# Second attention: products of q's rows, and of k's positions for the last two batches, on VectorE instead of GpSimd, at other steps

## The chip, the cores and the metric

The kernel runs on one core of a Trainium2 chip. The metric is the device time of one execution in microseconds (us), lower is better. The engines are called as in the profile: PE (TensorE, with PEld for its weight loads), ACT (ScalarE), DVE (VectorE), POOL (GpSimd) and SP (SyncE, which here issues most DMAs). Each engine works through its own list of instructions in order and waits at the head of the list until what that instruction needs is there.

## The reference

The input `x` has 4 batches of 512 positions with 128 features. There are two layers, each of the form

```
xn = layernorm(x)
s  = attention(xn)
g  = silu(ffn(xn))
x  = x + s * g
```

The first layer has a segmented linear attention with memory (16 heads of 64) and a mixture of 8 experts. The second layer, which the change touches, has 16 heads of 8 features and 16 "wavelength" channels:

```
Q, K, V = projections of xn, per head 8 features
for each channel w:
    scores = (Q * cos_pm[w]) @ (K * cos_pm[w])^T * scale     # times a cosine that is 1 here
    acc += softmax(scores) @ V * interference_weights[w]
s = (acc / 16) @ Wo + bo
```

followed by an expert layer with gelu (8 experts, the two best per position).

## The kernel before

All of it is one program: loads and first expert layer, first attention, second expert layer, second attention, and a path for large values that isn't taken here. The change lies in the second attention and in what is prepared for it.

**How the second attention computes.** The 16 channels differ only in a factor on the scores. So the kernel computes two exponential functions of the scores for every pair of positions (`e`, and its square), and adds the low powers of the scores (first, second, third), from which every channel's exponential is put together as a weighted sum. The part over pairs of positions is long: exponentials on ACT (`function1` with f = 0), squares on ACT or DVE (f = 1), and the sums over keys on PE (`acc`). The powers need no pairs: sums over keys of products of k's features (the "forms", `pl`) are multiplied with products of q's features (`first`, `second`, `third`, into `b`).

**The loop of `attn1`.** There are 64 steps, 16 per batch; step t of batch b is `i = 16 b + t`. A step takes one tile of 128 keys for four heads with all 512 queries. In each step PE sums over keys with the two functions of this step (`acc`, 16 matmuls), then computes the scores two steps ahead (`s`, 4 matmuls), then does one or two extra pieces of work. ACT computes the exponentials of the next step and evicts small results; the squares of the next step follow. The extra pieces are the preparation of the batch after this one (`prepare1`) and the mixing of the channels of this or the last batch (`sums1` with `den` and `inv`, `quotients1` with `mix` and `pr`, `bank1` with `b`, `output1` with `po`). Their matmuls are issued in one step, what follows on other engines (called `rest`) in the next; a `rest` may return a function that is done one step later still. All these instructions are pinned in the order in which the program writes them, engine by engine.

**Squares on DVE.** `RELIEVED` lists the steps (mod 16) whose second half of squares is done by DVE instead of ACT; the first tuple is for batches 0 to 2, the second for the last batch. The square of step i+1 is issued in step i. The functions of step 0 of batch 0 are done ahead, in `opening1`, which is called from within the second expert layer, before its last two groups of expert sums (`g`, line 966). For lack of other space they lie in `third1` and `first1[1]`.

**Preparation of k.** `tokens("k")` projects k with positions on partitions. DVE adds the bias (`tokk`), POOL copies the 8 features behind themselves (`twice`, 128 x 512) and multiplies them into `feat`, all products of two features, in two instructions of 128 x 2048 (line 1229). DVE's `cubes(m)` makes products of three features from it (lines 1311 to 1323) for four groups of heads; PE's `forms(m)` (`pl`) sums both. For batches 0 and 1 `tokens("k")` runs during the second expert layer; for batches 2 and 3 in steps 12 (PE) and 13 (the rest) of batches 0 and 1. There is one `feat`, and one set of cubes at a time (`feat3`).

**Products of q.** q's rows are written to DRAM in expanded form (`qe`, `qf`) and loaded again as `first`, `second` and `third`, with features on partitions, for two halves of the heads (mm = 0, 1). `quads1` multiplies `second` with `first` (line 1447) on POOL, in two instructions of 128 x 512 per half; `cubes1` then multiplies `first` with `second` and `third` with `second` on DVE (lines 1456, 1458), and `bank1` uses all three at steps 8 and 15. A table in `attn1` gives the steps at which each is loaded (`load`, `other`), squared (`two`) and cubed (`three`, `four`); a negative step lies in the batch before.

**Other work on POOL in the loop:** splitting k and q into three bf16 parts (`partk`, `leftk`, `partq`, `leftq`, ten instructions per batch of 0.6 to 1.6 us each), the squares of `tokq`, the gate (`th`, `g`), the sums of `pr`, and the output `y`. SP issues the writes of the parts and of q's expanded rows and all loads, in program order.

## Time and profile before

| | |
|---|---|
| time, median of 3 runs | 775.9 us (772.36 to 778.27) |
| the profiled execution | 776.21 us |
| its span, first to last instruction | 774.4 us |
| mean granted clock of PE | 0.986 |
| second attention's loop | 475.9 to 751.7 us, then the end |
| POOL, `second` (line 1447) | 32 instructions, 55.3 us |
| POOL, `feat` (line 1229), within the loop | 4 instructions, 17.7 us |
| DVE, `first` (line 1456) | 16 instructions, mean 1857 ns, shortest 1189 ns |

The profile is of one execution. A row of a group gives the line, engine and operation, out<-in by the program's names, the shapes and the count, then the busy time in us and the mean of one in ns, then how long the engine was idle before these instructions and what ended that. The timeline gives start and length in us and the idle time before in brackets. In the table by windows each line has the window, its length, the busy time and number of instructions of PE, PEld, DVE, ACT and POOL, the granted clock, the busy share of the DMA engines and GB/s.

### The profile page before, as it was taken

The numbers are of one execution on the slowest core, as the hardware profiler recorded it, in microseconds if no ns is written. First come the engines' busy times: TensorE is split into PE (matmuls) and PEld (weight loads), VectorE is DVE, ScalarE is ACT, GpSimd is POOL, SyncE is SP. The second block draws the span as 40 slices with busy tenths as digits, with TensorE's granted clock in tenths as the row PEclk, the third lists the DMA queues.
The fourth block names the chain that finished last, engine by engine and source line by source line (L and its number), as shares of the span: only waits on it lengthen the run. The fifth ranks groups of instructions, "written<-read, shape, count | busy, mean of one in ns | idle before, by whom it ended". The sixth has DMA issues, their size and how long they took to land. (4 is left out here: it accounts for less than half of the span.)

```text
span 774.4 us, 23667 instructions
## 1 busy us (share of the span) xinstructions
PE 727.4 (94%) x10060; PEld 437.9 (57%) x10060; DVE 523.2 (68%) x1111; ACT 489.3 (63%) x793; POOL 361.9 (47%) x378
## 2 busy tenths in 40 slices
PE   8999899999999989799999999999789987999997
PEld 4665577787787858666776774343234332432235
DVE  7775476656558766864455535877897699676964
ACT  4332666767668776544322227999688786879940
POOL 7660045555546435653063041734971776170650
PEclk9999999999999999999999999999899998999997
DMA  7830423213123121000013802667856393639200
GB/s 191 151 80 0 120 75 99 80 48 98 52 66 95 39 76 40 21 2 1 1 39 111 219 2 68 192 177 169 197 169 153 99 244 135 149 94 218 55 16 17
DMA packets 77745, 74.72 MB, mean 96 GB/s; under 512 B 41937, under 2 KB 66801, under 8 KB 74561
## 3 DMA queue, kind: packets, MB, share of 16 engines
q1 hardware_dynamic: 75568, 71.98, 35.6%
q0 software_dynamic: 1488, 0.90, 0.8%
q8 instruction: 81, 1.33, 0.8%
q10 hardware_dynamic: 576, 0.26, 0.1%
q14 instruction: 32, 0.25, 0.1%
HBM read 50.04 MB, written 23.07 MB: 94 GB/s over the span
## 5 line engine op out<-in xcount | busy, mean ns | idle before, releaser
L334 ACT ACTIVATE e<-s 128x1024 f32<-128x1024 f32 x126 | 123.5, 1048 | 25.9 <-PE s L331 25.1
L331 PE MATMUL acc<-e,strip 128*32 128x512 f32 x1008 | 127.6, 611 | 0.3 <-DVE e L1687 0.3
L334 ACT ACTIVATE e<-e 128x1024 f32<-128x1024 f32 x99 | 102.4, 1088 | 0.0
L334 ACT ACTIVATE h<-ph 128x1024 f32<-128x1024 f32 x32 | 32.8, 1025 | 84.2 <-PE ph L331 84.2
L769 POOL TENSOR_TENSOR t<-t,gate 128x512 f32<-128x512 f32 x32 | 40.8, 1275 | 72.1 <-DVE sums L768 65.7
L1447 POOL TENSOR_TENSOR second<-second,first 128x512 f32<-128x512 f32 x32 | 55.3, 1752 | 29.8 <-DMA second<-qf 22.8
L331 PEld LDWEIGHTS acc<-e,strip 128*32 128x32 f32 x1008 | 28.8, 111 | 71.1 <-issue 61.6
L331 PEld LDWEIGHTS eo<-w_out,h 128*128 128x128 f32 x512 | 60.7, 192 | 12.5 <-issue 9.6
L331 PE MATMUL eo<-w_out,h 128*128 128x128 f32 x512 | 63.4, 277 | 1.6 <-DVE g L966 1.3
L334 ACT ACTIVATE pj<-pp 128x512 f32<-128x512 f32 x64 | 38.3, 598 | 39.4 <-PE pp L331 39.1
L679 DVE SCALAR_TENSOR_TENSOR elu<-elu,up 128x512 f32<-128x512 f32 x60 | 48.9, 815 | 20.2 <-ACT up L334 20.1
L331 PE MATMUL ph<-xnT,w_in 128*128 128x512 f32 x128 | 60.3, 594 | 0.0
L731 POOL TENSOR_TENSOR t<-t,gate 128x512 f32<-128x512 f32 x32 | 41.4, 1295 | 39.9 <-DVE t L712 39.8
L966 DVE SCALAR_TENSOR_TENSOR g<-eo,gw,g 128x128 f32<-128x128 f32 x112 | 31.4, 342 | 40.1 <-PE eo L331 40.1
L1687 DVE TENSOR_TENSOR e<-e 128x1024 f32<-128x1024 f32 x27 | 42.0, 1556 | 19.1 <-ACT e L334 19.0
L770 POOL TENSOR_TENSOR t<-t,t 128x512 f32<-128x512 f32 x32 | 46.1, 1439 | 2.5
L331 PE MATMUL s<-q,k 64*128 64x512 bf16 x256 | 39.8, 382 | 2.9 <-ACT e L334 1.5
L331 PEld LDWEIGHTS <-k 64*128 64x128 bf16 x256 | 8.1, 94 | 58.9 <-issue 53.8
L334 ACT ACTIVATE elu<-pj 128x512 f32<-128x512 f32 x60 | 38.0, 633 | 0.1
L334 ACT ACTIVATE up<-pj 128x512 f32<-128x512 f32 x60 | 37.8, 630 | 0.0
L334 ACT ACTIVATE attT<-pa 128x128 f32<-128x128 f32 x128 | 25.1, 283 | 17.5 <-PE pa L780 17.5
L331 PE MATMUL pv<-l0Wv,xnT 128*128 128x512 f32 x64 | 34.6, 636 | 0.8 <-ACT vt L334 0.7
(288 smaller groups left out, 1561.0 us busy)
## 6 DMA issues: line engine op xcount, KB each, us to landing
vd<-vt SPq DMA_DIRECT2D x32, 256.0 KB
vone<-vd SPq DMA_DIRECT2D x64, 128.0 KB
first<-qe SPq DMA_DIRECT2D x8, 1024.0 KB
second<-qf SPq DMA_DIRECT2D x16, 512.0 KB
third<-qf SPq DMA_DIRECT2D x32, 256.0 KB
qf<-qT SPq DMA_DIRECT2D x64, 64.0 KB
k<-kd SPq DMA_DIRECT2D x16, 256.0 KB
q<-qd SPq DMA_DIRECT2D x16, 256.0 KB
```

Source lines behind the costliest of these rows:

```text
L331: return self.pin(self.nc.tensor.matmul(*args, **kw))
L334: return self.pin(self.nc.scalar.activation(*args, **kw))
L679: self.vec1(nc.vector.scalar_tensor_tensor(t, t, 1.0, up, ALU.min, ALU.add))
L731: nc.gpsimd.tensor_mul(t, t, self.gate)
L769: nc.gpsimd.tensor_mul(t, t, gate2)
L770: nc.gpsimd.tensor_add(t, t, seg[n]["t1"])
L966: self.vec1(v.scalar_tensor_tensor(acc[b][:, k, :], eo[:, k, :], w, acc[b][:, k, :], ALU.mult, ALU.add))
L1447: self.pool1(self.nc.gpsimd.tensor_mul(t[:, r], t[:, r], first[:, r]))
L1687: self.vec1(self.nc.vector.tensor_mul(t, src[pair], src[pair]))
```

## The change

`quads1` becomes one DVE instruction of 128 x 1024 per half instead of two POOL instructions of 128 x 512. It is now issued at the end of a step, ahead of `cubes1`, instead of near its start. Its steps become (1, 2) for batch 0 and (-1, 0) for the others in the first half of the heads, and (7, 9) in the second half for all batches. The second half's `first` is cubed at steps 9 and 10, and batch 0's second half is loaded at step 1 instead of 4. For batches 2 and 3 the copy into `twice` and the two products into `feat` run on DVE, the second of them one step later; for batches 0 and 1 they stay on POOL. The list of relieved steps of batches 0 to 2 becomes 0, 1, 5, 10, 11 instead of 1, 10, 11, 14, 15.

In DVE's list the square of step 0 of batch 0, `first<-third`, stands between the groups of `g` for experts 5 and 6 of the last batch.

```diff
-RELIEVED = ((1, 10, 11, 14, 15), (0, 1, 3, 4, 5, 7, 9, 10, 11, 13, 14, 15))
+RELIEVED = ((0, 1, 5, 10, 11), (0, 1, 3, 4, 5, 7, 9, 10, 11, 13, 14, 15))
...
-                self.pool1(nc.gpsimd.tensor_copy(twice[:, :, D1 : 2 * D1], t))
-                for at in (0, 4):
-                    self.pool1(nc.gpsimd.tensor_mul(
-                        feat[:, :, at : at + 4], bc(t, 2, 4), moved(twice, SECOND[at], 2, 4)
+                eng, pin = (nc.gpsimd, self.pool1) if b < 2 else (nc.vector, self.vec1)
+                pin(eng.tensor_copy(twice[:, :, D1 : 2 * D1], t))
+
+                def quads(at):
+                    pin(eng.tensor_tensor(
+                        feat[:, :, at : at + 4], bc(t, 2, 4), moved(twice, SECOND[at], 2, 4),
+                        ALU.mult,
                     ))
                 now["squares" + w], now["twice_k"] = feat[:, :, 0], twice
+                quads(0)
+                return lambda: quads(4)
...
-        t, first = self.second1[mm], self.first1[mm]
-        for r in (2 * half, 2 * half + 1):
-            self.pool1(self.nc.gpsimd.tensor_mul(t[:, r], t[:, r], first[:, r]))
+        two = slice(2 * half, 2 * half + 2)
+        t = self.second1[mm][:, two]
+        self.vec1(self.nc.vector.tensor_mul(t, t, self.first1[mm][:, two]))
...
                 for mm, load, two, other, three, four in (
-                    (0, -5, (-3, -2), 1, (0, 2), (4, 6)) if fb else
-                    (0, 0, (2, 3), 1, (4, 5), (6, 7)),
-                    (1, 1, (4, 5), 9, (7, 9), (11, 13)) if fb else
-                    (1, 4, (6, 7), 9, (8, 9), (11, 13)),
+                    (0, -5, (-1, 0), 1, (0, 2), (4, 6)) if fb else (0, 0, (1, 2), 1, (3, 4), (6, 7)),
+                    (1, 1, (7, 9), 9, (9, 10), (11, 13)),
                 ):
...
-                for which in quads.get(i, []):
-                    self.quads1(*which)
                 for which in loads.get(i, []):
                     self.loaded1(*which)
...
                     first, second = e0, function(i + 1, 1, e0)
+                for which in quads.get(i, []):
+                    self.quads1(*which)
                 for which in cubes.get(i, []):
                     self.cubes1(*which)
...
-                        rest(evict[0](ps) if evict else ps)
+                        after = rest(evict[0](ps) if evict else ps)
+                        if after:
+                            after()
```

## The prediction

> **What bounds the kernel now.** I read the page first, then the second attention (475.9 us to the end) by batch, then what TensorE waits for there, then the timeline around the two longest waits. In the page, parts 1 and 4:

> ```profile
> PE 727.4 (94%) x10060; PEld 437.9 (57%) x10060; DVE 523.2 (68%) x1111; ACT 489.3 (63%) x793; POOL 361.9 (47%) x378
> PE acc L331 6%; ACT e L334 4%; DMA second<-qf 4%; PE b L331 2%; POOL feat L1229 2%; DVE feat L1323 2%; PE s L331 2%; SPq L343 1%; PE mix L331 1%; POOL second L1447 1%; DVE feat L1311 1%; PE oute L331 1%; PE po L331 1%; PE pl L331 1%; DVE inv L1508 1%
> ```

> TensorE is the busy engine, yet the chain that ends last leaves it for `second<-qf`, POOL's `feat` and `second`, and DVE's `feat`. The table by batch (window, length, busy time of PE, PEld, DVE, ACT, POOL, clock, DMA) shows where:

> ```profile
> 475.90:539.50 63.60, 62.54 (x743) 23.09 (x741) 49.41 (x63) 61.14 (x75) 30.47 (x25) 1.00 0.71 179
> 539.50:617.30 77.80, 70.75 (x796) 28.14 (x788) 62.74 (x70) 61.53 (x74) 51.12 (x32) 0.96 0.60 157
> 617.30:695.50 78.20, 71.27 (x792) 27.12 (x784) 65.28 (x70) 60.44 (x73) 46.52 (x32) 0.96 0.62 156
> 695.50:751.70 56.20, 55.32 (x474) 16.85 (x472) 43.75 (x47) 46.79 (x52) 22.59 (x15) 1.00 0.42 99
> ```

> Batches 1 and 2 have some 7 us each in which PE is idle. The waits of PE in 539 to 696 us (total, times, longest):

> ```profile
> PE mix L331 <- DVE pr L1533: 6.8, 3, 4.7
> PE pl L331 <- DVE feat L1323: 6.0, 3, 4.5
> PE ptq L331 <- DVE inv L1508: 1.1, 1, 1.1
> ```

> That is 13.9 us, all on DVE. Why DVE is late stands in the timeline (start, us; in brackets the idle time before it):

> ```profile
> 535.88 2.52 POOL L1447 TENSOR_TENSOR second<-second,first 128x512 f32<-128x512 f32 x2 [9.85 <-DMA second<-qf]
> 539.04 9.38 POOL L1229 TENSOR_TENSOR feat<-tokk 128x2048 f32<-128x2048 f32 x2
> 540.06 4.66 DVE L1456 TENSOR_TENSOR first<-first,second 128x1024 f32<-128x1024 f32 x1
> 548.45 2.28 DVE L1311 TENSOR_TENSOR feat<-tokk,feat 128x1024 f32<-128x1024 f32 x1 [3.13 <-POOL feat L1229]
> 550.65 1.30 DVE L1315 COPY feat<-tokk 128x128 f32<-128x128 f32 x1
> 556.74 1.95 PE L331 MATMUL pl<-feat,strip 128*32 128x129 f32 x32 [4.54 <-DVE feat L1323]
> ...
> 636.27 0.21 DVE L1315 COPY feat<-tokk 128x128 f32<-128x128 f32 x1
> 650.59 2.67 PE L331 MATMUL mix<-inv,to_mix 64*128 64x512 f32 x4 [4.74 <-DVE pr L1533]
> ```

> POOL stands at its head until a load lands, so `tokk` and `feat` behind it start at 538.4. And DVE's own instructions stretch while POOL works: the same copy takes 0.21 and 1.30 us, a 1024-wide product 1.2 or 4.66.

> [...] the reciprocal from PSUM keeps 1.75 us beside POOL's work. [...]

> **The change, part by part.** Durations are of the profiled execution: 776.2 us, its span 774.4; the median of three runs, 775.9, is 0.3 below it.

> 1. Work moved. POOL loses 32 `second` (55.3 us), 4 `feat` of batches 2 and 3 (17.7) and 2 copies (1.2): 74 us. DVE gains 16 products of 1024 at 1.14 (the spacing of such rows back to back) = 18.2, 4 of 2048 at 2.29 = 9.2, 2 copies. A copy of 512 is not shown on DVE: [...] at most 0.69 (L1209, as wide, with two inputs); I take 0.5. Together 28.4 us.

> 2. What DVE gets back. From 616.92 to 651.05 DVE is never idle: 34.1 us. The same instructions at their undisturbed durations (e 1.14, two `first` 2.28, `strip` 0.6, three sets of cubes of 2.73, two halves of `inv` 3.34, `tokq` 0.6, `bank` 0.66, `third` 1.2, `pr` 1.2) are 19.2. So POOL costs it 15 us there, and batch 1 is alike (538.9 to 576.1).

> 3. Batch 1 walked anew from step 0 at 539.5. The two `second` at the end of steps 15 and 0 need a load that landed by 535.8, before step 15's end, so DVE doesn't wait. After `e`, `second`, `first`, `strip` (its matmul ends at 543.0) DVE is free at about 543.6, against 548.45 for its cubes before. Cubes: 2.73, plus 3 as POOL's five steps on k run then; to 549.3. `inv`, `first`, `inv`: 554.5. Second cubes, partly beside POOL's steps on q: 558.2. `tokq`, `bank`, `e` (now relieved here), `third`: 561.8. Third cubes 564.5, `pr` 565.7. PE, unstalled, wants these at 553, 559 and 566. So all three waits fall away, the last by 0.3 us only; I leave 0.5 us as a remainder for both batches. Gain: 13.9.

> 4. The clock. Half speed was granted in 554.6 to 561.5 and 650.2 to 657.0. Of the first 2.1 us lay inside the wait that ends at 556.7, of the second 0.4; without these waits such windows cost the half of that, 1.3 us. Steps 14 and 15 of batch 2 took 9.83 us, in batch 1 8.39, with `e` stretched to 2.33: 1.4 back. These two cancel.

> 5. RELIEVED. In batch 0 ACT sets the pace of steps 0 to 7 (31.7 us, ACT busy 39.0 of 40 in 480 to 520): square 5 on DVE takes 1.0 off. In batches 1 and 2 five squares stay five; ACT, 65 us per batch, has room at steps 14 and 15.

> 6. The opening. Step 0 is now relieved in batch 0 too, and DVE's order has this square ahead of the last two groups of `g` (L966):

> ```profile
> 472.17 1.94 ACT L334 ACTIVATE third<-s 128x1024 f32<-128x1024 f32 x2
> 472.30 1.12 DVE L966 SCALAR_TENSOR_TENSOR g<-eo,gw,g 128x128 f32<-128x128 f32 x4 [3.11 <-PE eo L331]
> 474.08 1.12 DVE L966 SCALAR_TENSOR_TENSOR g<-eo,gw,g 128x128 f32<-128x128 f32 x4 [0.66 <-PE eo L331]
> 475.35 0.61 PE L331 MATMUL s<-q,k 64*128 64x512 bf16 x4 [1.31 <-DVE g L966]
> ```

> The square waits for the exponential's second half, 474.1; then 1.14, then 1.12 twice: `g` ends at 477.4 instead of 475.2, and PE's scores, ACT's next exponentials and all after them wait for it. Loss 2.2.

> 7. Step 14 of batches 0 and 1. Between `tokk` and `pr` DVE now has the copy, `feat`, `third`, `feat`. From the end of `ptk`: 0.12 wait, 0.62, 0.5, 2.2, 1.15, 2.2, then `pr` 1.2: 8.0. The second pair of `mix` needs the PSUM buffers that `pr` frees, and PE is there after 2.39+1.07 and 2.39 = 5.85 us; the two matmul pairs follow the two `pr`, which takes back some 0.3. Loss 1.9 each, 3.8. It can be 1.3 (first `pr` alone decides) to 2.6 (copy at 0.69, POOL in between).

> 8. SP. Batch 0's second loads go out at 479.5, behind `third`, instead of 498.05. The writes of k's parts queue behind 2 MB that took 11.9 us before (498.05 to 509.95), so POOL's `partq` starts near 495 instead of 488.6 and `tokq`'s squares end near 502; DVE sums them at 504.2. Nothing, or up to 2 us if later. In return POOL's wait of 10.20 us for this load, and DVE's of 1.76 behind it, end.

> 9. Batch 3: 4 `second` leave POOL and DVE gets 4.6 us, against stretched rows of about the same sum (2.30, 2.29, 3.86 for two). Nothing.

> Sum: -13.9 - 1.0 + 2.2 + 3.8 + 0.5 = -8.4, so 776.2 becomes 767.8.

> **Rivals.**
> - The walk is too kind: the cubes still meet POOL's ten steps on k and q, whose order I guess, and half the 13.9 us stays. For it: the margin of 0.3 us. Against: POOL has 74 us less. 767.8 + 7 = 775.
> - DVE becomes the bound. At `mix` of step 6 in batches 1 and 2, PE waits longer than before: DVE has 3.4 us more ahead of it (two `second`, square 5), and [...] each wait would grow by that: 13.9 kept, 6.8 added, with 2.2, 3.8 and -1.0: 788. It decides from where POOL gives back less than 3.4 us per batch; overall the change turns to a loss once less than 2.5 us per batch is regained. For it: DVE already at 62.7 and 65.3 us of 78. Against: 7 of the 15 us, at POOL's share of removed work, should go.
> - Items 6 and 7 cost nothing, the opening being covered and ACT's two added squares holding PE at step 14 anyway: 762. Against: ACT is ahead there, it waited 2.33 us for scores at step 12.
> - That the change doesn't do what it says: excluded by the instruction order, which has the products on DVE.

> **Numbers.** Chances: forecast 0.55, half kept 0.18, DVE bound 0.12, cheaper 0.15. Predicted 767.8. The forecast alone spans 763 to 772 (item 7's ends, item 8, the remainder); to the others, the range is 759 to 782. About 1% (7.8 us) can be told from no change: faster by more means under 768.1, which is half of the forecast and nearly all of the cheaper case, 0.46; slower by more means over 783.7, most of the DVE-bound case, 0.11; within, 0.43.

> **What would show it.** POOL's lines of `second` gone; DVE `first` near 1.2 us mean instead of 1.86; no PE `pl<-DVE feat` or `mix<-DVE pr` wait over 1 us at steps 2 to 6 of batches 1 and 2, which take about 70 us each; a new PE `mix<-DVE pr` wait near 2 us at step 14 of batches 0 and 1; PE's scores waiting 3.5 us for DVE `g` before step 0. Wrong: waits at step 6 that are as long as now, or DVE waiting for `second<-qf` with `strip` and the cubes behind it.

## The result, and the profile after

The changed kernel takes 771.99 us (median of 16 runs, 766.18 to 774.73); the kernel before, run beside it as often, takes 778.3 (772.36 to 782.64). The ratio is 0.992, 95% interval 0.9892 to 0.9947: 6.3 us faster by the medians, where 8.4 were forecast. The profiled execution took 772.95 us, its span 771.1, at a mean clock of 0.981 (before: 0.986).

Parts 1 and 4 of the page after:

```profile
PE 729.7 (95%) x10060; PEld 439.4 (57%) x10060; DVE 522.8 (68%) x1133; ACT 489.6 (63%) x793; POOL 292.7 (38%) x340
PE acc L331 9%; ACT e L334 5%; PE b L331 3%; PE s L331 3%; PE pl L331 2%; PE po L331 1%; PE den L331 1%; PE mix L331 1%; DVE feat L1231 1%; PE oute L331 1%; DMA kd<-partk 1%; DVE feat L1328 1%; PE pf L331 1%; POOL partk L1283 1%; DVE feat L1316 1%; DVE third L1463 1%
```

POOL is 69 us less busy, and its `feat` and `second` and the load `second<-qf` have left the chain. DVE, which took those products over, is as busy as before (523.2, now 522.8): its instructions beside POOL's got shorter by as much as it was given. The batches (columns as before):

```profile
481.64:548.70 67.06, 64.39 (x742) 23.08 (x740) 57.24 (x70) 61.21 (x74) 18.00 (x15) 0.97 0.68 169
548.70:622.72 74.02, 70.57 (x796) 27.47 (x789) 61.41 (x77) 61.11 (x74) 25.34 (x19) 0.98 0.66 165
622.72:691.96 69.24, 67.69 (x788) 26.73 (x781) 57.53 (x73) 61.17 (x74) 23.36 (x19) 1.00 0.69 176
691.96:748.15 56.19, 55.31 (x472) 16.86 (x472) 43.81 (x52) 46.80 (x52) 14.61 (x10) 1.00 0.43 99
```

Batch 0 is 3.4 us longer than before, batch 1 3.8 shorter, batch 2 8.9 shorter, batch 3 the same. PE's waits from 470 to 760 us (total, times, longest) say which waits are left and which are new:

```profile
PE mix L331 <- DVE pr L1538: 6.0, 4, 1.9
PE s L331 <- DVE g L966: 3.5, 1, 3.5
PE s L331 <- ACT e L334: 1.9, 5, 0.5
```

The waits for `feat` (6.0 us) are gone, and so is the wait of 4.7 for `pr`. Four waits of 1.2 to 1.9 us for `pr` are there: step 14 of batches 0 and 1, forecast, and step 6 of batches 1 and 2, for which the forecast had left 0.5 us in all. The wait for `g` before step 0 is the forecast one.

With the start of each step taken from its first `acc`, the two profiled executions differ as follows. A term forecast is an item of the prediction.

| stretch | before, us | after, us | difference | forecast |
|---|---|---|---|---|
| start to the first exponential of the loop (`third<-s`) | 472.17 | 475.26 | +3.1 | 0 |
| from there to step 0 (item 6) | 3.72 | 6.38 | +2.7 | +2.2 |
| step 0 of batch 0 | 4.34 | 6.49 | +2.15 | 0 |
| step 6 of batch 0 (item 5) | 4.04 | 3.10 | -0.9 | -1.0 |
| step 14 of batch 0, of batch 1 (item 7) | 3.53, 3.26 | 5.99, 6.04 | +5.2 | +3.8 |
| steps 2 to 7 of batch 1 | 32.9 | 26.3 | -6.6 | items 3 and 4 |
| steps 2 to 7 of batch 2, and 14, 15 | 42.7 | 33.8 | -8.9 | together -13.4 |
| all else | | | 0.0 | 0 |

The sum is -3.3, the difference of the spans (774.4 and 771.1). From here on, a half-speed window is a stretch in which the trace grants PE half the clock. The first row is code that the change does not touch: in the execution after there are such windows of 3.41 us each at 11.7, 284.8 and 318.9 us, in the one before none up to there. That they make up the whole 3.1 us is not shown. Without this row the sum is -6.4, close to the difference of the medians.

**The opening**, timeline of after:

```profile
475.26 1.94 ACT L334 ACTIVATE third<-s 128x1024 f32<-128x1024 f32 x2
477.23 1.23 DVE L1692 TENSOR_TENSOR first<-third 128x1024 f32<-128x1024 f32 x1 [4.96 <-ACT third L334]
478.37 2.15 DVE L966 SCALAR_TENSOR_TENSOR g<-eo,gw,g 128x128 f32<-128x128 f32 x8
480.67 1.04 PE L331 MATMUL s<-q,k 64*128 64x512 bf16 x4 [3.54 <-DVE g L966]
481.64 1.93 PE L331 MATMUL acc<-third,strip 128*32 128x512 f32 x8
```

`g` stands behind the square and ends 5.3 us after the start of the exponential, as forecast (before: 3.0). What was not forecast is in the last two rows: four matmuls `s` take 1.04 us where they took 0.61, and eight `acc` 1.93, where 16 take 1.92 at full speed. The windows from 475.86 and from 479.28 on (length, then busy time of PE, PEld, DVE, ACT, POOL, the granted clock, DMA):

```profile
475.86:479.28 3.42, 1.27 (x12) 1.08 (x10) 2.05 (x5) 2.28 (x3) 0.00 (x0) 1.00 0.00 0
479.28:486.10 6.82, 5.43 (x24) 0.89 (x24) 2.47 (x6) 3.12 (x4) 0.00 (x0) 0.50 0.18 52
```

PE was busy for 1.27 of 3.42 us, and in the 6.8 us after that it was granted half speed. That is step 0's 2.15 us; that it belongs to the wait is what e10_filled tests below.

**Step 14 of batch 1**, timeline of after:

```profile
609.60 2.29 DVE L1231 TENSOR_TENSOR feat<-tokk 128x2048 f32<-128x2048 f32 x1
611.81 1.28 DVE L1463 SCALAR_TENSOR_TENSOR third<-second,count,third 128x1024 f32<-128x1024 f32 x1
613.00 2.29 DVE L1231 TENSOR_TENSOR feat<-tokk 128x2048 f32<-128x2048 f32 x1
615.20 1.28 DVE L1538 TENSOR_TENSOR pr<-bank,mix 128x512 f32<-128x512 f32 x2
615.94 1.72 PE L331 MATMUL mix<-inv,to_mix 64*128 64x512 f32 x4 [1.92 <-DVE pr L1538]
617.17 1.28 DVE L1538 TENSOR_TENSOR pr<-bank,mix 128x512 f32<-128x512 f32 x2 [0.69 <-PE mix L331]
```

The wait, 1.92, is the forecast 1.9 (in batch 0 it is 1.40). But the four matmuls take 1.72 us here and 1.03 in the kernel before: the second two need the buffer that the second `pr` frees, at 616.5. The step grows by both and a little more, 2.8 us.

**Step 6 of batch 1**: SP's DMA issues, then the timeline of POOL, DVE and PE.

```profile
552.13 0.59 SPq L343 DMA_DIRECT2D first<-qe  x1
552.77 1.24 SPq L343 DMA_DIRECT2D second<-qf  x2
556.10 5.07 SPq L343 DMA_DIRECT2D kd<-partk  x5
```
```profile
567.94 0.77 POOL L1283 CAST partq<-qT 128x512 bf16<-128x512 f32 x1 [7.16 <-ACT e L334]
569.71 2.19 DVE L1316 TENSOR_TENSOR feat<-tokk,feat 128x1024 f32<-128x1024 f32 x1
572.57 3.31 DVE L1328 TENSOR_TENSOR feat<-tokk,feat 128x256 f32<-128x256 f32 x3
576.53 1.72 PE L331 MATMUL mix<-inv,to_mix 64*128 64x512 f32 x4 [1.53 <-DVE pr L1538]
```

SP sends 2 MB of loads ahead of the writes of k's parts. In the trace the loads land at 560.6, 563.0 and 565.4, the writes of the first part from 565.9 to 567.8. `partq` reuses the buffer that these writes read, so POOL starts on q at 567.94, 19.2 us into the batch (the bracket names ACT's `e`; in batch 0 the same instruction is shown to wait 8.62 us for `kd<-partk`). POOL's six steps on q then lie on DVE's third cubes, which take 6.1 us instead of 2.7, and `pr` behind them is late. In the kernel before the loads were sent at the same step, but PE stood for 4.5 us at step 2. The writes were sent from 555.1 us on, the last load landed at 555.9, so the writes had hardly anything to wait for.

DVE's groups in the second attention, mean in ns:

```profile
L1452 DVE TENSOR_TENSOR second<-second,first 128x1024 f32<-128x1024 f32 x16 | 24.9, 1558 | 0.0
L1461 DVE TENSOR_TENSOR first<-first,second 128x1024 f32<-128x1024 f32 x16 | 19.4, 1211 | 0.0
L1231 DVE TENSOR_TENSOR feat<-tokk 128x2048 f32<-128x2048 f32 x4 | 9.2, 2289 | 0.1
```

### The profile page after: what moved, and what is told of

It reads as the page before. It is cut to its first block, busy times and chain, and to the rows that moved or that the text cites. A ratio compares the mean times of both kernels' runs of the same rounds, so it can differ in the third digit from the quotient of the medians.

```text
span 771.1 us, 23617 instructions
## 1 busy us (share of the span) xinstructions
PE 729.7 (95%) x10060; PEld 439.4 (57%) x10060; DVE 522.8 (68%) x1133; ACT 489.6 (63%) x793; POOL 292.7 (38%) x340
## 5 line engine op out<-in xcount | busy, mean ns | idle before, releaser
L334 ACT ACTIVATE e<-s 128x1024 f32<-128x1024 f32 x126 | 123.1, 1042 | 24.7 <-PE s L331 23.9
L331 PE MATMUL acc<-e,strip 128*32 128x512 f32 x1008 | 124.9, 604 | 0.3 <-DVE e L1692 0.3
L334 ACT ACTIVATE e<-e 128x1024 f32<-128x1024 f32 x100 | 103.1, 1080 | 0.0
L334 ACT ACTIVATE h<-ph 128x1024 f32<-128x1024 f32 x32 | 32.8, 1025 | 84.2 <-PE ph L331 84.2
L331 PEld LDWEIGHTS eo<-w_out,h 128*128 128x128 f32 x512 | 60.7, 192 | 12.5 <-issue 9.7
L331 PEld LDWEIGHTS acc<-e,strip 128*32 128x32 f32 x1008 | 28.7, 109 | 68.3 <-issue 59.2
L331 PE MATMUL eo<-w_out,h 128*128 128x128 f32 x512 | 63.4, 277 | 1.6 <-DVE g L966 1.4
L334 ACT ACTIVATE pj<-pp 128x512 f32<-128x512 f32 x64 | 38.3, 598 | 39.9 <-PE pp L331 39.4
L331 PE MATMUL ph<-xnT,w_in 128*128 128x512 f32 x128 | 60.3, 594 | 0.0
L966 DVE SCALAR_TENSOR_TENSOR g<-eo,gw,g 128x128 f32<-128x128 f32 x112 | 31.4, 343 | 36.3 <-PE eo L331 36.3
L331 PE MATMUL s<-q,k 64*128 64x512 bf16 x256 | 41.1, 389 | 5.8 <-DVE g L966 3.5
L1692 DVE TENSOR_TENSOR e<-e 128x1024 f32<-128x1024 f32 x26 | 34.5, 1327 | 15.2 <-ACT e L334 15.2
L331 PEld LDWEIGHTS <-k 64*128 64x128 bf16 x256 | 8.2, 94 | 62.8 <-issue 60.2
L1543 POOL TENSOR_TENSOR pr<-pr,pr 128x512 f32<-128x512 f32 x14 | 20.6, 1489 | 49.6 <-DVE pr L1538 49.6
L334 ACT ACTIVATE elu<-pj 128x512 f32<-128x512 f32 x60 | 38.0, 634 | 0.1
L334 ACT ACTIVATE up<-pj 128x512 f32<-128x512 f32 x60 | 37.9, 631 | 0.0
L334 ACT ACTIVATE attT<-pa 128x128 f32<-128x128 f32 x128 | 25.1, 283 | 18.7 <-PE pa L780 18.7
L331 PE MATMUL pv<-l0Wv,xnT 128*128 128x512 f32 x64 | 35.5, 652 | 0.8 <-ACT vt L334 0.7
```

The source lines that it names most:

```text
L331: return self.pin(self.nc.tensor.matmul(*args, **kw))
L334: return self.pin(self.nc.scalar.activation(*args, **kw))
L966: self.vec1(v.scalar_tensor_tensor(acc[b][:, k, :], eo[:, k, :], w, acc[b][:, k, :], ALU.mult, ALU.add))
L1543: self.nc.gpsimd.tensor_add(self.prod1[b, m], self.prod1[b, m], t)
L1692: self.vec1(self.nc.vector.tensor_mul(t, src[pair], src[pair]))
```

## The experiments

All times are medians; the kernel before was run on the same chip beside each. The ratio is the recorded one with its interval; it differs from the ratio of the two medians by up to 0.3% (most for e11_old_list). What follows reads the waits and steps from one trace of each kernel.

| kernel | us | ratio to before, 95% interval |
|---|---|---|
| changed kernel | 771.99 | 0.992 (0.9892 to 0.9947) |
| e1_load2 | 768.69 | 0.9871 (0.9836 to 0.9905) |
| e2_feat_alone | 774.54 | 0.9955 (0.9935 to 0.9975) |
| e3_second_alone | 769.02 | 0.9899 (0.9865 to 0.9934) |
| e4_three | 759.28 | 0.9752 (0.972 to 0.9784) |
| e5_opening | 766.22 | 0.985 (0.9796 to 0.9904) |
| e6_step14 | 768.76 | 0.9874 (0.9838 to 0.991) |
| e8_relieved | 766.03 | 0.9836 (0.9796 to 0.9877) |
| e9_second_two | 757.76 | 0.973 (0.9696 to 0.9763) |
| e10_filled | 770.06 | 0.9893 (0.9872 to 0.9914) |
| e11_old_list | 766.51 | 0.9865 (0.9818 to 0.9912) |

### Which half of the change carries the gain: e2_feat_alone and e3_second_alone

e2_feat_alone is the changed kernel with `quads1` as before (POOL, old steps, called where it was), the old loads and the old RELIEVED. e3_second_alone has one line:

```diff
-                eng, pin = (nc.gpsimd, self.pool1) if b < 2 else (nc.vector, self.vec1)
+                eng, pin = nc.gpsimd, self.pool1
```

> Half of the change: feat and its copy of batches 2 and 3 on DVE, while the products of q's rows (second) stay on POOL at their old steps, with the old list of relieved steps. Theory: PE's wait of 4.5 us for feat at step 2 of batch 1 goes, since POOL's 9.4 us of feat are no longer ahead of the cubes; step 6 of batch 1 and 2 keeps part of its wait, since second on POOL still stretches DVE; step 14 of batches 0 and 1 costs 2.5 us each; the opening stays at 3.7 us. Sum: -6.0 (waits for feat) - 2 (a part of the 6.8 for pr) + 5.2 = about -3, ratio 0.996. Rival (the removed feat is what carries the whole gain): batches 1 and 2 as short as in the changed kernel, and with no loss in the opening ratio 0.989. Rival (second at POOL's head is what matters): waits at steps 2 and 6 stay, ratio over 1.002.

> The other half: second on DVE at the new steps and the new relieved steps, while feat of all batches stays on POOL. Theory: POOL no longer stands at its head for a load, so its feat starts some 4 to 5 us earlier and the cubes at step 0 to 2 no longer wait, or wait under 1 us; step 14 of batches 0 and 1 returns to 3.3 to 3.5 us; the opening loses 2.7 us; feat on POOL still stretches DVE at the end of each batch. Sum: about -10 of waits - 1.0 + 2.7 = -8, ratio 0.990, as good as the whole change or better. Rival (the 9.4 us of POOL's feat carry the stretch): the wait for feat at step 2 stays at 2 to 4 us, ratio 0.998 or more, since DVE has more to do beside it.

In both traces the waits for `feat` are gone: steps 2 to 4 of batches 1 and 2 have the same lengths as in the changed kernel, up to 0.6 us. So each half alone removes that wait, and their gains (0.45% and 1.0%) do not add (0.8%). `second` alone is at least as fast as the whole, as far as the overlapping intervals tell. Its remaining waits are 2.1 us each at step 6 of batches 1 and 2, its steps 14 have none. e2 meets what DVE loses beside POOL. Batch 1, step 14:

```profile
608.66 9.91 POOL L1452 TENSOR_TENSOR second<-second,first 128x512 f32<-128x512 f32 x4 [2.41 <-PE s L331]
614.10 3.35 DVE L1231 TENSOR_TENSOR feat<-tokk 128x2048 f32<-128x2048 f32 x1
618.10 2.67 PE L331 MATMUL mix<-inv,to_mix 64*128 64x512 f32 x4 [4.48 <-DVE pr L1538]
```

The product that takes 2.29 us alone takes 3.35, and the wait is 4.48 instead of 1.92; steps 14 took 8.8 and 11.3 us where 6.0 each were expected. Both theories' ratios (0.996 and 0.990) are met, but e2's by luck. In its trace steps 0 to 13 of batch 1 and the whole of batch 2 are 18.9 us shorter than before, where 8 were expected, and steps 14 and 15 of batches 0 and 1 are 17.0 us longer, where 5.2 were expected. e2's first rival, that the removed `feat` carries the whole gain, is right on these stretches (in the changed kernel they are 15.5 us shorter) and misses only the price at step 14. Its second rival and e3's fall: the waits for `feat` are gone in both traces.

### The wait at step 6: e1_load2

```diff
-                    (1, 1, (7, 9), 9, (9, 10), (11, 13)),
+                    (1, 2, (7, 9), 9, (9, 10), (11, 13)),
```

> The changed kernel with one number different: the second half of each batch's first/second loads goes out at step 2 instead of step 1. Theory (what is left of the wait at step 6 of batches 1 and 2 comes from POOL's steps on q, which start late because the writes of k's parts queue behind 2 MB of loads, and then meet the third cubes): partq of batch 1 starts near 560 us instead of 567.9, the three third cubes take near 2.7 us instead of 6.1, PE's waits of 1.5 and 1.2 us for pr at step 6 are gone, about 4 us less than the changed kernel, ratio to before 0.987. Rival (DVE is simply full there): step 6 of batches 1 and 2 stays at 5.3 to 5.6 us wherever partq runs, ratio 0.992. A second rival: the later load lands after step 7 and DVE's second product waits for it, slower than the changed kernel by 2 to 4 us.

SP's issues and the rows of POOL and DVE in batch 1:

```profile
556.35 4.46 SPq L343 DMA_DIRECT2D kd<-partk  x5
...
561.91 0.53 SPq L343 DMA_DIRECT2D first<-qe  x1
562.49 1.24 SPq L343 DMA_DIRECT2D second<-qf  x2
```
```profile
561.01 0.61 POOL L1283 CAST partq<-qT 128x512 bf16<-128x512 f32 x1 [0.58 <-ACT qT L334]
572.11 1.22 DVE L1316 TENSOR_TENSOR feat<-tokk,feat 128x1024 f32<-128x1024 f32 x1
573.59 1.09 DVE L1328 TENSOR_TENSOR feat<-tokk,feat 128x256 f32<-128x256 f32 x3
```

The writes now go ahead of the loads and land within 2.5 us, `partq` starts at 561.0, the third cubes take 2.6 us, and step 6 takes 3.25 us in both batches (5.64 and 5.27 in the changed kernel); PE has no wait from 548 to 600 us. The theory holds; the rivals of a full DVE and of a load that comes too late fall. The price was not foreseen: in batch 0 `partq` moves forward too, to 492.2, and steps 5 and 6 are 1.3 us longer together. This comes only with the square of step 5 on DVE: with that square on ACT, the two steps take 6.42 us with the early load (e8_relieved) and with the late one (e11_old_list). In this trace steps 14 of batches 0 and 1 are 1.7 and 1.0 us longer as well, each with a window of half-speed clock behind its wait (in batch 1 from 614.08 to 617.49, clock 0.50, with PE idle for 1.92 of the 3.41 us ahead of it), of which more below.

### The opening: e5_opening, and what makes the half-speed clock: e10_filled

```diff
-            elif pair and i % 16 in RELIEVED[i // 16 == B - 1]:
+            elif pair and i and i % 16 in RELIEVED[i // 16 == B - 1]:
```

> The changed kernel with the square of step 0 of batch 0 on ACT again, all else equal. Theory: from the first exponential (third<-s) to step 0 it takes 3.7 us again instead of 6.4, PE's wait of scores for g is 1.3 instead of 3.5 us, and ACT's square delays nothing that is not regained within batch 0: 2.2 to 2.7 us less, ratio 0.989. Rival (ACT, which sets the pace of steps 0 to 7 of batch 0, gives the gain back): scores wait 1.3 us but steps 0 to 7 take 1 to 2 us longer, ratio 0.991 to 0.992.

Timeline of PE:

```profile
478.38 0.61 PE L331 MATMUL s<-q,k 64*128 64x512 bf16 x4 [1.31 <-DVE g L966]
478.92 1.07 PE L331 MATMUL acc<-third,strip 128*32 128x512 f32 x8
```

From `third<-s` to step 0 it takes 3.73 us again, and step 0 takes 4.34 again: 2.65 and 2.15, 4.8 us in the trace, about twice the expected 2.2 to 2.7: the half-speed window went with the wait. Batch 0's steps 1 to 7 are as in the changed kernel, so ACT gives nothing back. The median is 5.8 us lower than the changed kernel's, but it is of four runs and the intervals touch, so the 4.8 us rest on the trace.

Within each of the twelve traces, all starts of half-speed windows lie on a grid of 3.413 us (in the changed kernel 479.34, 578.33 and 752.41 are 29 and 51 grid stretches apart). I took PE's idle time in every grid stretch of the second attention from 468 to 743 us which itself ran at full speed, and whether the next one ran at half:

| idle in the stretch of 3.41 us | stretches | next at half speed |
|---|---|---|
| 1.9 us or more | 14 | 14 |
| 1.4 to 1.9 | 12 | 6 |
| less than 1.4 | 911 | 0 |

e10_filled puts that to the test. It leaves the wait for `g` alone and only gives PE something to do in it, after the call of `ffn1` in `run`:

```diff
                 self.ffn1(first, between, True)
+                spare = psum.tile([P, 2, S], F32, name="spare", tag="w", bufs=3)
+                now = self.now1[0]
+                for r in range(16):
+                    rows = slice(r % 2 * HALF, r % 2 * HALF + HALF)
+                    self.mm1(
+                        spare[:, r % 2], lhsT=now["k", 0][rows, 0, 0:P],
+                        rhs=now["q", 0][rows, 0], start=True, stop=True,
+                    )
```

> The changed kernel with 16 throwaway matmuls on PE behind the last eo, in a PSUM tile that nobody reads: PE has some 2.4 us of work within its wait of 3.5 us at the opening, everything else and the output are unchanged. In the ten traces up to here every half-clock window of the second attention lies behind an idle stretch of PE. Theory (the idle stretch itself makes the window): the wait for g still ends about 5.3 us after the first exponential starts, third<-s to step 0 stays at 6.4 us, but no window follows and step 0 takes 4.3 us instead of 6.5: 2 us less than the changed kernel, ratio 0.989. Rival (the window is drawn by something else, load or time, and the idle stretch only happens to be near): step 0 stays at 6.0 to 6.5 us, ratio 0.992 or more.

Timeline of PE, and the windows around it (columns as above):

```profile
477.03 1.90 PE L331 MATMUL spare<-q,k 64*128 64x512 bf16 x16
480.64 0.61 PE L331 MATMUL s<-q,k 64*128 64x512 bf16 x4 [1.71 <-DVE g L966]
481.17 1.07 PE L331 MATMUL acc<-third,strip 128*32 128x512 f32 x8
```
```profile
480.50:487.30 6.80, 6.66 (x50) 2.34 (x50) 3.76 (x6) 6.19 (x8) 0.76 (x2) 1.00 0.58 135
```

`s` still starts 5.4 us after the exponential, but no window follows, and step 0 takes 4.34 us. In the four traces that have the wait unfilled (the changed kernel, e1, e3 and e6) one followed each time: the first eight `acc` take 1.93, 1.62, 1.93 and 1.93 us there, and 1.07 here. So it is PE's idle time, and not the place in the program, that makes the window. This is one trace, and the filled stretch still had 1.4 us idle, at the edge of the table's middle row; without the 1.90 us of filling it would have had 3.3, by that sum. The time (0.9893) overlaps with the changed kernel's and does not show the 2 us by itself; in this trace batch 0 lost as much again at step 14, where a wait of 2.2 us stood just ahead of a window of its own (541.8).

### Step 14: e6_step14

The second `feat` product is marked and run after the mixing chunk's `pr` instead of ahead of it:

```diff
+                held = [f for f in late if hasattr(f, "after")]
                 for f in late:
-                    f()
+                    if f not in held:
+                        f()
...
                 late = [f for f in [rest(x) for rest, x in ready] if f]
+                for f in held:
+                    f()
```

> The changed kernel with one change of order: at step 14 of batches 0 and 1 the second feat product of DVE is issued after pr and not ahead of it. Theory: PE's waits for pr there (1.40 and 1.92 us) go, steps 14 take some 3.5 instead of 6.0 us, 5 us less than the changed kernel, ratio 0.986. Rival (ACT's two added squares hold PE at step 14 anyway, or the product only moves on to third of step 15): steps 14 and 15 together shrink by less than 1.5 us each, ratio 0.990 or more.

Steps 14 take 3.78 and 3.83 us (5.99 and 6.04), PE has no wait there, and step 15 is 0.4 and 0 longer: 4.0 us saved of the 5 that the theory names, and more than the rival allows. The time, 0.9874, agrees with it, though the intervals overlap. The waits of step 6 stayed and were 2.2 and 2.0 us in this trace; behind the one in batch 2 a window of 6.83 us at half speed made steps 6 and 7 3.8 us longer.

### The list of relieved steps: e8_relieved and e11_old_list

```diff
-RELIEVED = ((0, 1, 5, 10, 11), (0, 1, 3, 4, 5, 7, 9, 10, 11, 13, 14, 15))
+RELIEVED = ((1, 10, 11, 14, 15), (0, 1, 3, 4, 5, 7, 9, 10, 11, 13, 14, 15))
```

> The changed kernel with the list of relieved steps as it was before (1, 10, 11, 14, 15 in place of 0, 1, 5, 10, 11); products on DVE as in the changed kernel. Theory: opening back to 3.7 us (-2.5), step 6 of batch 0 back to 4.0 us (+1.0), the squares 14 and 15 on DVE add to the waits for pr at step 14 of batches 0 and 1 (1.1 us each), while the squares 0 and 5 off DVE let the third cubes of batches 1 and 2 start 2.3 us earlier and take most of the waits of 1.5 and 1.2 us at step 6: sum -2.5 + 1.0 + 2.2 - 3 = about -2, ratio 0.989. Rival (the new list is what makes room for the change): step 14 of batches 0 and 1 over 8.5 us and ratio over 0.996.

e8_relieved's interval, of four runs, lies just below the changed kernel's: with the products on DVE and nothing else mended, the new list costs more than it brings. The opening and step 0 give 4.8 us back, step 6 of batch 0 takes 0.95 more, steps 14 and 15 of batches 0 and 1 5.6 more together (7.86 and 7.17 at step 14), and steps 6 and 7 of batches 1 and 2 3.1 less. The signs are the theory's and the rival falls, but two sizes are off and cancel: -4.8 for -2.5 at the opening, +5.6 for +2.2 at the end of the batches. From the first exponential of the loop to batch 3 this trace is 2.3 us shorter than the changed kernel's, against the theory's -2. The medians say -6; of the rest, 2.7 us in the traces lie in batch 3 and behind it, which the edit does not touch (there are 6.83 us of half-speed clock at 752.4 in the changed kernel and none there in e8_relieved).

e11_old_list makes the same edit to e9_second_two (below), where POOL computes `feat`.

> e9_second_two with the list of relieved steps as it was before (1, 10, 11, 14, 15), which has the square of step 0 of batch 0 on ACT anyway. Theory: squares 14 and 15 on DVE meet POOL's feat of 7.5 us and add to the waits for pr at step 14 of batches 0 and 1 (1 to 2.4 us each and half-clock windows behind them, as in e8_relieved), step 6 of batch 0 is 1.0 us longer: 4 us slower than e9_second_two or more, ratio 0.978 or over. Rival (without feat DVE has room at steps 14 and 15, and gains at steps 0 to 6 of batches 1 and 2): within 2 us of e9_second_two, ratio 0.971 to 0.976.

It is 1.35% slower than e9_second_two by the ratios (1.15% by the medians; the intervals are apart), nearly all of it at step 14 of batch 0 (10.2 us instead of 3.7), the step after it and, by 1.4 us, batch 1. The timeline there:

```profile
533.81 8.40 POOL L1231 TENSOR_TENSOR feat<-tokk 128x2048 f32<-128x2048 f32 x2
534.36 4.17 DVE L1696 TENSOR_TENSOR e<-e 128x1024 f32<-128x1024 f32 x1 [1.30 <-ACT e L334]
538.45 4.84 DVE L1467 SCALAR_TENSOR_TENSOR third<-second,count,third 128x1024 f32<-128x1024 f32 x1
```

Two DVE rows of 1.2 us take 9.0 beside POOL's `feat`. At step 14 of batch 1 no such wait came (3.25 us), against the expectation; why is open. So relieving steps 0 and 5 instead of 14 and 15 is right in this kernel, where POOL has `feat`, but the square of step 0 of batch 0 must stay with ACT.

### All losses taken out: e4_three and e9_second_two

e4_three has the edits of e1_load2, e5_opening and e6_step14 together; e9_second_two is e4_three with the line of e3_second_alone.

> The changed kernel with the three losses that its trace shows taken out: the later load of e1_load2; the square of step 0 of batch 0 on ACT again; at step 14 of batches 0 and 1 the second feat product of DVE issued after pr instead of before it. Theory: opening back to near 3.7 us (-2.5), step 14 back to near 3.5 us (-5), step 6 near 3.5 to 4 us (-4): some 10 us less than the changed kernel, ratio to before 0.980. If the losses only move (DVE full, the feat product after pr now delays e and third of the next step): under 4 us less, ratio 0.987 to 0.992.

> e4_three with feat and its copy of batches 2 and 3 back on POOL: second on DVE, the later load, the square of step 0 of batch 0 on ACT. It asks what moving feat is worth once everything else is mended. Theory (feat on DVE only costs DVE time at step 14, and POOL, whose head no longer waits for a load, has room for its 7.5 us there): same as e4_three or up to 3 us faster, ratio 0.971 to 0.976. Rival (POOL's feat beside step 14 and 15 still stretches DVE's e, pr and third and makes the next batch late): waits of PE for pr at step 6 or for feat at steps 0 to 2 come back, 3 us or more slower than e4_three, ratio over 0.979.

The three edits alone gain 0.49, 0.70 and 0.46% over the changed kernel, together 1.7%: they add, as far as intervals of 0.3 to 0.5% on either side can tell. In us that is some 13, where the theory had 10; its terms had no half-speed windows in them. e9_second_two's theory (0.971 to 0.976) is met. e9_second_two's batches:

```profile
480.14:544.37 64.23, 62.15 (x743) 22.97 (x741) 51.19 (x66) 61.22 (x75) 27.26 (x18) 1.00 0.71 177
544.37:611.65 67.28, 67.28 (x796) 27.07 (x788) 57.01 (x74) 60.76 (x74) 31.78 (x22) 1.00 0.71 181
611.65:679.66 68.01, 67.02 (x789) 27.02 (x781) 57.73 (x73) 60.82 (x74) 27.42 (x21) 1.00 0.70 179
679.66:735.83 56.17, 55.29 (x471) 16.87 (x472) 44.33 (x52) 46.77 (x52) 14.59 (x10) 1.00 0.41 99
```

PE is busy in 67.28 of 67.28 us of batch 1, and the clock is at full speed in all four. The two kernels are 1.5 us apart, their intervals overlap: once `second` is off POOL and the list is the new one, it makes no difference that can be told who computes `feat`. Both are faster than the kernel before (by 2.5 and 2.7%) and than the changed one.

## Why the forecast came out as it did

The forecast, 767.8 from an execution of 776.2, was -8.4 us; the medians say -6.3. Direction and mechanism held; four terms of the sum were mis-sized: the remainder of item 3, and items 4, 6 and 7. For item 4, these are the two half-speed windows of the kernel before in batches 1 and 2, each with the stretch ahead of it (columns as before):

```profile
551.20:554.61 3.41, 1.00 (x36) 0.49 (x32) 3.41 (x4) 2.52 (x3) 3.41 (x4) 1.00 1.04 235
554.61:561.44 6.83, 4.70 (x48) 2.17 (x48) 6.83 (x7) 2.34 (x4) 6.46 (x7) 0.50 0.50 156
646.75:650.16 3.41, 0.00 (x0) 0.00 (x0) 3.41 (x4) 3.41 (x4) 2.90 (x3) 1.00 0.26 98
650.16:656.99 6.83, 6.40 (x22) 1.73 (x24) 6.76 (x10) 0.14 (x1) 2.50 (x2) 0.50 0.42 140
```

- **Item 1, work moved.** `feat` took 2289 ns. The 2.29 us in the forecast was shown by no row of before; an estimate from that trace, two rows of 1024 at their spacing of 1.14 us back to back, would be 2.28. The copy took 428 ns where I took 500; the trace of before had that number in operations of the same width with one input (`gate`, L579 and L580, 426 and 428 ns). `second` took 1558 ns on the mean against 1140: some of it lies beside POOL's work, 2.30 or 2.31 us beside `pr`. So DVE took on 35 us, not 28.4.
- **Item 2, what DVE gets back.** Right, and more than the rival that DVE becomes the bound allowed: `first` fell from 1857 to 1211 ns, the squares from 1556 to 1327, and the whole of DVE stayed at 523 us with 35 us more to do. That rows are shorter with less of POOL's work beside them is measured; what lengthens them is not shown.
- **Item 3, batches 1 and 2.** The waits at steps 2 to 4 fell away as walked. The step that failed is "third cubes 564.5, `pr` 565.7", and the remainder of 0.5 us hung on it: it put POOL's chain on q beside the second cubes, before 18.7 us into the batch. The chain starts at 19.2 us, and the waits at step 6 remain with 1.53 and 1.16 us; against 3.25 us without them (e1_load2) step 6 costs 4.4 us more in both batches. Item 8 had the cause, the writes of k's parts behind 2 MB, but only for batch 0, where steps 7 to 13 show no loss from it.
- **Item 4, the clock.** It said that windows at half speed would stay without the waits, and cost 1.3 us more. The two left in the trace of after from the first exponential to the end of batch 3 stand behind waits of PE: 6.83 us from 479.34 on behind the 3.54 for `g`, and 3.41 us from 578.33 on behind the 1.53 at step 6 of batch 1. The long waits took their windows of 6.83 us with them, and steps 2 to 7 of batch 1 and the whole of batch 2 gained 15.5 us where 13.4 were forecast (13.9 less the remainder of 0.5, and nothing for the clock). That these two are so close is in part luck: the remainder was 3.9 us too small, and the windows that went are worth an estimated 5.5 us (half of the 11.1 us for which PE was busy in them).
- **Item 5.** 1.0 forecast, 0.94 measured. Its "65 us per batch" for ACT is DVE's number; ACT's are 60.4 to 61.5, and no term hangs on it.
- **Item 6, the opening.** The delay of `g` was right (2.2; 2.7 in the trace). The term lacks the window that the wait draws: 2.15 us more, 4.8 in all, as e5_opening shows by removing both and e10_filled by removing the window alone.
- **Item 7, step 14.** The walk of DVE is right to 0.1 us (in batch 1, from the end of `ptk` to the end of the two `pr` 8.1 us; 8.0 forecast), and so is the wait there; in batch 0 it is 0.5 shorter. Wrong is "which takes back some 0.3": the second pair of matmuls costs 0.7 more. 5.2 instead of 3.8.
- **Item 9.** Batch 3 is as long as before to 0.01 us.

Sum of the terms measured: -15.5 - 0.9 + 4.8 + 5.2 = -6.4. Of the rivals, "items 6 and 7 cost nothing" falls with the traces of e5_opening and e6_step14; the one that half the gain stays had its mechanism in part (the third cubes met POOL's steps on q, for 4.4 us instead of 7, while the rest gained more than forecast), and DVE as the bound falls with e1_load2, where DVE has the same work and PE no wait at step 6.

## What to carry to other kernels

A wait of the matmul engine that is taken out, or put in, can be worth more than its length: look whether half-speed windows stand behind it, and add them to the term (2.15 us at the opening here, 1.6 at step 7 of batch 1; nothing behind the waits at step 14 of the changed kernel). When a stall goes, transfers that it used to give time to come next: walk the DMA queue for every repetition of the loop, not for the first one (here the writes of k's parts behind the loads: 4.4 us at step 6 of batches 1 and 2). Two parts of a change that remove the same wait are not to be priced by their sum (0.45 and 1.0% here, 0.8% together); the part that is worth nothing on top of the other is best left where its engine has room.
